# A two-layer graph attention kernel: the residual-plus-bias add on VectorE, and one product of the second projection moved

## The chip, the cores and the metric

The kernel runs on 1 core of one Trainium2 chip. The metric is the device time of a whole execution in microseconds (us). Engines are written as the profile does: PE is TensorE (PEld its weight loads), DVE is VectorE, ACT is ScalarE, POOL is GpSimd, SP is SyncE, which here only issues DMAs.

## The reference, cut to what matters

32 graphs of 512 nodes with 512 features each. The input is normalised and rectified, goes through two graph attention layers under a mask made of the adjacency matrix, and is added back to the input:

```python
h = jnp.maximum(_layernorm(x, axis=-1), 0.0)
x = x + gnn(adj, h, ...)                        # the residual

def gat_layer(x, mask, W, a_src, a_dst, bias, concat):
    xl = (x @ W).reshape(B, N, H, F)            # projection
    asrc = einsum('bnhf,hf->bnh', xl, a_src); adst = ...
    e = leaky_relu(asrc[:, :, None, :] + adst[:, None, :, :], 0.2)
    attn = softmax(where(mask[..., None], e, NEG_INF), axis=1)
    out = einsum('bsdh,bshf->bdhf', attn, xl)   # gather
    return (heads joined, or their mean) + bias

mask = (adj > 0) | eye(N)
h = elu(gat_layer(x, mask, W1, ..., b1, concat=True))    # 4 heads of 256
out = gat_layer(h, mask, W2, ..., b2, concat=False)      # 1 head of 512
```

The part that the change touches is `x + out + b2` at the end of each graph, and the order of the matrix products of `h @ W2`.

## The kernel before, in words

All data are float32 but the masks. The 512 nodes of a graph lie as 4 tiles of 128 partitions. The kernel is a pipeline over the graphs: iteration i of the main loop (L457) does, in this order on PE, the first projection of graph i+1 (`project1`, L306, `pxl`), then the second gather of graph i-1 (`gather2`, L414, `po` of L427) and the second projection of graph i (`project2`, L371, `pxm`), and then the first gather of graph i+1 (`gather1`, L325, `po` of L333). Between these products stand small transposes: of the normalised x of graph i+2 (`pht`, L187), of masks (`pm`, L208), and of softmax rows (`pas`, `prr`, L227). PE's order is the program's own (L456). DVE, ACT, POOL and SP get theirs from the scheduler, which works on what depends on what and may place an instruction well ahead of the line that wrote it. Each engine and SP's queue of DMAs run their instructions strictly in that order.

The attention of a head (class `Soft`) goes through all engines. `first(h)` (L254) makes the scores on ACT (L263), masks them on DVE (L266), takes exponentials on ACT (L270) and ends in a column `r`. `turn(h)` (L282) transposes `r` on PE (`prr`, L227), copies it out of PSUM on DVE (`rrr`, L229), writes it to DRAM (`drr`, L231) and reads it back spread over all partitions (`orr`, L233). `second(h)` (L285) makes the probabilities `p` in four passes on DVE (L292), four exponentials on ACT (L296) and two minima with the mask on DVE (L300). During one `gather2` and `project2` the heads 0 to 3 of graph i+1 go through these steps one behind the other.

`project2` multiplies by a Strassen-like scheme: 14 products (m, n), with n from 1 to 7 and m the half of the rows, each of 8 PE instructions. Products with the same accumulator (`pxm_0a`, `pxm_0b`, `pxm_0g`, `pxm_1a`, ...) add up in the same PSUM bank, and after each product the bank is read out before the next product adds to it: n = 1, 5, 6 by a copy on ACT (L399), n = 4 by a copy on ACT (L401), the others by an addition on DVE (L404). Their order is the list in L389. So product (1, 7), which adds to `pxm_1a`, waits until ACT has copied `pxm_1a` after (1, 6); (0, 4) waits until DVE has read `pxm_0a` after (0, 7); and (1, 4) until DVE has read `pxm_1a` after (1, 7).

All small transposes share two PSUM tiles in turn (tag `tp`, bufs=2), so a transpose waits until the one two places ahead has been copied out.

In `gather2` the x of the graph is loaded a second time in two tiles `xr` of two node tiles each (L421), POOL adds the bias of the second layer to each (L422, 128x1024), DVE adds the gather's PSUM result to it (L432), and SP stores it (L433). The `xr` tiles have two buffers, so a load waits for the store of the graph before.

Of the kernel before, what the change touches and what calls it, by code (L numbers as in the profile page):

```python
# [8 lines left out]
F32 = mybir.dt.float32  # L9
# [3 lines left out]
OP = mybir.AluOpType  # L13
# [3 lines left out]
P = 128  # L17
# [11 lines left out]
def tile_gat(  # L29
# [30 lines left out]
    nc = tc.nc  # L60
    B, N, D = x.shape
# [3 lines left out]
    NT = N // P  # L65
# [7 lines left out]
    work = ctx.enter_context(tc.tile_pool(name="work", bufs=2))  # L73
# [22 lines left out]
    b2_sb = const.tile([P, DO], F32, name="b2_sb")  # L96
# [57 lines left out]
    def load(b):  # L154
        XT[b] = []
        for t in range(NT):
            xt = work.tile([P, D], F32, tag="x", name=f"x{b}_{t}", bufs=4)
            nc.sync.dma_start(xt, x[b, t * P : (t + 1) * P, :])
            XT[b].append(xt)

    def load_adj(b):
        ADJ[b] = []
        for t in range(NT):
            a = work.tile([P, N], I32, tag="adj", name=f"adj{b}_{t}", bufs=2)
            nc.sync.dma_start(a, adj[b, t * P : (t + 1) * P, :])
            ADJ[b].append(a)
# [179 lines left out]
    def x2(b):  # L346

        if b < B - 1:
            return xl2

        return bass.AP(
            tensor=xl.tensor, offset=xl.offset, ap=[xl.ap[0], [DO + 2, NT], [1, DO + 2]]
        )

    def sums2(b):

        h1 = H1.pop(b)
        M = N // 2
        a11, a12 = h1[:, :KH, :M], h1[:, KH:, :M]
        a21, a22 = h1[:, :KH, M:], h1[:, KH:, M:]  # L360
        hs = work.tile([P, 3, KH, M], F32, tag="hs", name=f"hs{b}", bufs=1)
        s1, s2, s4 = (hs[:, i] for i in range(3))
        nc.vector.tensor_add(s1, a21, a22)
        nc.vector.tensor_sub(a21, a11, a21)
        nc.vector.tensor_sub(s2, s1, a11)
        nc.vector.tensor_sub(s4, a12, s2)
        LEFT[b] = {1: a11, 2: a12, 3: s4, 4: a22, 5: s1, 6: s2, 7: a21}
# [3 lines left out]
    def project2(b):  # L371
        left = LEFT.pop(b)
        v = x2(b)
        bank = {}

        def product(m, n, acc, first):
            if first:
                bank[m, acc] = psum.tile([P, 512], F32, tag="mm", name=f"pxm{b}_{m}{acc}", bufs=6)
            ps = bank[m, acc]
            for k in range(KH):  # L380
                nc.tensor.matmul(  # L381
                    ps[:, :W2H], left[n][:, k, m * P : (m + 1) * P], RIGHT[n][:, k, :],
                    start=(first and k == 0), stop=(k == KH - 1), skip_group_check=True,
                )

        def block(r, c, m):
            return v[:, 2 * r + m, c * W2H : (c + 1) * W2H]

        for m, n in (  # L389
            (0, 1), (0, 2), (0, 5), (1, 1), (0, 6), (1, 2), (1, 5),  # L390
            (0, 7), (1, 6), (0, 3), (1, 7), (0, 4), (1, 3), (1, 4),
        ):
            acc = {1: "a", 2: "g", 5: "b", 6: "a", 7: "a", 3: "b", 4: "a"}[n]
            product(m, n, acc, n in (1, 2, 5))
            ps = bank[m, acc][:, :W2H]

            if n in (1, 5, 6):
                to = {1: (0, 0), 5: (1, 1), 6: (0, 1)}[n]
                nc.scalar.activation(block(*to, m), ps, AF.Copy)  # L399
            elif n == 4:  # L400
                nc.scalar.activation(block(1, 0, m), ps, AF.Copy)  # L401
            else:
                to = block(*{2: (0, 0), 7: (1, 1), 3: (0, 1)}[n], m)
                nc.vector.tensor_add(to, ps, to)  # L404
            yield

    def cols2(b):
# [3 lines left out]

        return cols

    def gather2(b):  # L414
        p = PS2.pop(b)
        v = x2(b)
        for d in range(NT):
            if d % 2 == 0:
                xr = work.tile([P, 2, D], F32, tag="xr", name=f"xr{b}_{d}", bufs=2)
                for j in range(2):  # L420
                    nc.sync.dma_start(xr[:, j, :], x[b, (d + j) * P : (d + j + 1) * P, :])  # L421
                nc.gpsimd.tensor_tensor(  # L422
                    xr, xr, b2_sb[:, None, :].to_broadcast([P, 2, D]), op=OP.add
                )
            ps = psum.tile([P, 512], F32, tag="mm", name=f"po2{b}_{d}", bufs=6)
            for s in range(NT):
                nc.tensor.matmul(  # L427
                    ps, p[:, s, d * P : (d + 1) * P], v[:, s, 1 : DO + 1],
                    start=(s == 0), stop=(s == NT - 1),
                )  # L430
            to = xr[:, d % 2, :]
            nc.vector.tensor_tensor(to, ps, to, op=OP.add)  # L432
            nc.sync.dma_start(out[b, d * P : (d + 1) * P, :], to)  # L433
            yield

    def step(g):

        if g is not None:
            next(g, None)

    def rest(g):
        for _ in g or ():
            pass
# [9 lines left out]
    def second_layer(b):  # L453
        return Soft(b, 2, cols2(b), lambda h, p: PS2.__setitem__(b, p))

    with tc.manual_schedule(engines={mybir.EngineType.PE}):  # L456
        for i in range(-1, B + 1):  # L457

            front = i + 2 < B
            nm = norm(i + 2) if front else None  # L460
            if front:
                load(i + 2)
                load_adj(i + 2)
                step(nm)
            s1 = None
            if i + 1 < B:
                s1 = Soft(i + 1, 1, cols1, lambda h, p, b=i + 1: PS1.__setitem__((b, h), p))
                mt = turned_masks(i + 1)
                for n, _ in enumerate(project1(i + 1)):
                    if n == 0 and late:  # L470
                        late.turn(0)
                        late.second(0)
                    step(mt)
                    if n == 2 and 0 <= i:
                        sums2(i)
                    if n == 3:
                        s1.columns(0)
                    if n == 4:
                        s1.rows(0)
                    if n == 5:  # L480
                        s1.first(0)
                    if n == 7:
                        s1.columns(1)
                        s1.first(1)
            else:
                if i < B:
                    sums2(i)
                    late.turn(0)
                late.second(0)
            late = None  # L490
            last = i == B - 1


            plan = {}
            if s1:
                plan = {
                    1: lambda: s1.rows(1),
                    3: lambda: (s1.turn(0), s1.first(2)),
                    4: lambda: s1.second(0),
                    9: lambda: (s1.turn(1), s1.first(3)),  # L500
                    10: lambda: s1.second(1),
                    13: lambda: s1.turn(2),
                    14: lambda: s1.second(2),
                    16: lambda: s1.turn(3),
                }
            g2 = gather2(i - 1) if i >= 1 else iter(())
            c2 = project2(i) if 0 <= i < B else iter(())
            order = [g2] * 4 + [c2] * 14
            if last:
                order = [g2] * 2 + [c2] * 14 + [g2] * 2  # L510
            for n, g in enumerate(order, 1):
                next(g, None)
                if n in plan:
                    plan.pop(n)()
                if n in (2, 6, 10, 14):
                    step(nm)
                if last and n == 16:
                    late = second_layer(i)
                    late.columns(0)
                if last and n == 17:  # L520
                    late.rows(0)
                    late.first(0)
            rest(nm)
            if last:
                late.turn(0)
            if 0 <= i < B and not last:
                late = second_layer(i)
                late.columns(0)
            if i + 1 < B:
                for n, _ in enumerate(gather1(i + 1)):  # L530
                    if n == 1:
                        s1.second(3)
                    if n == 2 and late:
                        late.rows(0)
                        late.first(0)
                    if n == 4 and front:
                        masks(i + 2)
# [29 lines left out]
```

## Time and profile before

| what | us |
|---|---|
| median of 3 runs | 3373.64 (3365.79 to 3383.51) |
| the profiled execution | 3373.38 |
| its span, first to last instruction | 3371.6 |
| PE busy | 3184.9 (94% of the span) |
| DVE busy | 2324.9 (69%) |
| ACT busy | 1791.2 (53%) |
| POOL busy | 218.9 (6%) |
| mean share of full TensorE clock granted | 0.973 |

[...] Below, "iteration g" is the stretch from the first matmul of the second gather of graph g to that of graph g+1; in it `project2` works on graph g+1 and the heads of graph g+2 go through their steps. Idle time of the other engines costs nothing unless PE waits for what they do late.

### The profile page before, as it was taken

The numbers are of one execution on the slowest core, as the hardware profiler recorded it, in microseconds if no ns is written. First come the engines' busy times: TensorE is split into PE (matmuls) and PEld (weight loads), VectorE is DVE, ScalarE is ACT, GpSimd is POOL, SyncE is SP. The second block draws the span as 40 slices with busy tenths as digits, with TensorE's granted clock in tenths as the row PEclk, the third lists the DMA queues.
The fourth block names the chain that finished last, engine by engine and source line by source line (L and its number), as shares of the span: only waits on it lengthen the run. The fifth ranks groups of instructions, "written<-read, shape, count | busy, mean of one in ns | idle before, by whom it ended". The sixth has DMA issues, their size and how long they took to land.

```text
span 3371.6 us, 35481 instructions
## 1 busy us (share of the span) xinstructions
PE 3184.9 (94%) x12032; PEld 2158.0 (64%) x12032; DVE 2324.9 (69%) x5099; ACT 1791.2 (53%) x3873; POOL 218.9 (6%) x102
## 2 busy tenths in 40 slices
PE   5899999999999999999999999999999999999986
PEld 4566676676666666666666676666666666666654
DVE  6677676677776677666677766676766776667762
ACT  2555655455555555555545555555554455555551
POOL 0000000000000000000000000000000000000000
PEclk8899999999999999999999999999999999999998
DMA  5112222222222222222222322122322222221121
GB/s 178 49 56 79 91 94 80 70 73 79 91 94 85 72 67 79 91 94 82 69 72 73 94 87 83 58 82 85 94 85 66 73 76 91 85 80 52 66 72 47
DMA packets 121462, 269.38 MB, mean 80 GB/s; under 512 B 15552, under 2 KB 22592, under 8 KB 121280
## 3 DMA queue, kind: packets, MB, share of 16 engines
q1 hardware_dynamic: 121280, 267.12, 24.7%
q8 instruction: 94, 1.54, 0.2%
q14 instruction: 88, 0.72, 0.1%
HBM read 232.53 MB, written 34.54 MB: 79 GB/s over the span
## 4 chain that ended last, share of the span: by engine, by line
PE 49%; DMA 19%; ACT 15%; DVE 14%; issue 1%; SPq 0%; POOL 0%; ACTq 0%; DVEq 0%
PE po L333 26%; PE pxl L313 12%; ACT l L263 6%; ACT l L270 6%; DMA oas<-das 6%; DMA orr<-drr 5%; PE pxm_1a L381 5%; DVE p L300 4%; DVE p L292 3%; DVE l L266 3%; DMA adj<-in_adj_dram 3%; PE pxm_0a L381 2%; DMA das<-ras 2%; DMA drr<-rrr 2%; PE pxm_1b L381 2%
## 5 line engine op out<-in xcount | busy, mean ns | idle before, releaser
L313 PE MATMUL pxl<-w_sb,ht 128*128 128x258 f32 x4096 | 933.9, 384 | 2.3 <-DMA w_sb<-in_L_gnn_W_dram 2.3
L333 PE MATMUL po<-p,xl 128*128 128x512 f32 x2048 | 889.3, 593 | 0.0
L266 DVE CUSTOM_DVE_ANT_0 l<-l,mt 128x512 f32<-128x512 f32 x640 | 462.4, 745 | 575.8 <-ACT l L263 573.6
L313 PEld LDWEIGHTS pxl<-w_sb,ht 128*128 128x128 f32 x4096 | 768.6, 191 | 127.0 <-issue 14.8
L333 PEld LDWEIGHTS po<-p,xl 128*128 128x128 f32 x2048 | 387.1, 190 | 473.3 <-issue 443.5
L263 ACT ACTIVATE l<-oas,sc 128x512 f32<-128x512 f32 x640 | 432.8, 710 | 267.4 <-DMA oas<-das 265.6
L296 ACT ACTIVATE p<-p,lo 128x512 f32<-128x512 f32 x640 | 436.1, 717 | 250.2 <-DVE p L292 249.3
L292 DVE SCALAR_TENSOR_TENSOR p<-orr,lo 128x512 f32<-128x512 f32 x640 | 447.9, 746 | 99.0 <-DMA orr<-drr 97.1
L270 ACT ACTIVATE l<-l,low 128x512 f32<-128x512 f32 x640 | 454.7, 711 | 104.8 <-DVE low L266 104.8
L427 PE MATMUL po<-xl,p 128*128 128x512 f32 x1024 | 461.8, 597 | 19.8 <-DVE p L300 19.8
L317 ACT ACTIVATE xl<-pxl 128x258 f32<-128x258 f32 x512 | 188.7, 381 | 535.7 <-PE pxl L313 535.1
L300 DVE TENSOR_TENSOR p<-p,m 128x1024 f32<-128x1024 f32 x320 | 439.0, 1393 | 1.2 <-ACT p L296 1.1
L422 POOL TENSOR_TENSOR xr<-xr,b_sb 128x1024 f32<-128x1024 f32 x64 | 185.5, 2898 | 2592.4 <-DMA drr<-rrr 1128.2
L427 PEld LDWEIGHTS po<-xl,p 128*128 128x128 f32 x1024 | 188.6, 191 | 231.9 <-issue 202.7
L381 PE MATMUL pxm_1a<-w_sb,h 128*128 128x257 f32 x768 | 214.9, 428 | 88.3 <-ACT xl L399 88.3
L339 ACT ACTIVATE e<-po,b_sb 128x512 f32<-128x512 f32 x256 | 170.3, 677 | 162.2 <-PE po L333 159.1
L381 PEld LDWEIGHTS pxm_1a<-w_sb,h 128*128 128x128 f32 x768 | 159.8, 212 | 121.3 <-ACT xl L399 95.4
L381 PE MATMUL pxm_0a<-w_sb,h 128*128 128x257 f32 x768 | 200.3, 406 | 4.5 <-ACT xl L399 4.2
L341 DVE SCALAR_TENSOR_TENSOR h<-po,b_sb,e 128x512 f32<-128x512 f32 x256 | 191.2, 747 | 7.8 <-PE po L333 0.5
L381 PEld LDWEIGHTS pxm_0a<-w_sb,h 128*128 128x128 f32 x768 | 159.7, 209 | 49.5 <-issue 14.7
L340 DVE TENSOR_SCALAR e<-e 128x512 f32<-128x512 f32 x256 | 107.6, 421 | 65.8 <-ACT e L339 65.7
L381 PE MATMUL pxm_0b<-w_sb,hs 128*128 128x257 f32 x512 | 121.9, 380 | 0.0
(77 smaller groups left out, 2330.9 us busy)
## 6 DMA issues: line engine op xcount, KB each, us to landing
orr<-drr SPq DMA_DIRECT2D x160, 512.0 KB
x<-in_x_dram SPq DMA_DIRECT2D x128, 256.0 KB
adj<-in_adj_dram SPq DMA_DIRECT2D x128, 256.0 KB
xr<-in_x_dram SPq DMA_DIRECT2D x128, 256.0 KB
oas<-das SPq DMA_DIRECT2D x64, 512.0 KB
out_dram<-xr SPq DMA_DIRECT2D x128, 256.0 KB
oas<-das SPq DMA_DIRECT2D x32, 256.0 KB
w_sb<-in_L_gnn_W_dram SPq DMA_DIRECT2D x8, 512.0 KB
```

The costliest lines, as they stand in the source:

```text
L263: nc.scalar.activation(e, self.asr[i][:, j, :], AF.Prelu, bias=ad[:, d : d + 1], alpha=SLOPE)
L266: nc.vector.tensor_tensor_reduce(out=e, in0=e, in1=MASKT[self.b][:, d, :], scale=-1.0, scalar=BIG, op0=OP.add, op1=OP.min, accum_out=low[: ...
L270: nc.scalar.activation(e, e, AF.Exp, bias=low[:, d : d + 1], scale=-1.0, accum_out=tot[:, d : d + 1])
L292: nc.vector.scalar_tensor_tensor(p[:, u, :], rr[:, 0, :], lo[:, 0, j, u : u + 1], rr[:, 1, :], op0=OP.add, op1=OP.max,)
L296: nc.scalar.activation(p[:, u, :], p[:, u, :], AF.Exp, bias=lo[:, 1, j, u : u + 1])
L300: nc.vector.tensor_tensor(pp, pp, MASK[self.b][:, t : t + 2, :], op=OP.min)
L313: nc.tensor.matmul(ps[:, :W], ht[:, k, t * P : (t + 1) * P], w1_sb[:, k, h, :], start=(k == 0), stop=(k == KT - 1),)
L317: nc.scalar.activation(xl[:, t, h, :], ps[:, :W], AF.Copy)
L333: nc.tensor.matmul(ps, xl[:, s, h, 2 + f * P : 2 + (f + 1) * P], p[:, s, :], start=(s == 0), stop=(s == NT - 1),)
L341: nc.vector.scalar_tensor_tensor(H1[b][:, g, :], ps, bias, e, op0=OP.add, op1=OP.max)
L381: nc.tensor.matmul(ps[:, :W2H], left[n][:, k, m * P : (m + 1) * P], RIGHT[n][:, k, :], start=(first and k == 0), stop=(k == KH - 1), skip_ ...
L427: nc.tensor.matmul(ps, p[:, s, d * P : (d + 1) * P], v[:, s, 1 : DO + 1], start=(s == 0), stop=(s == NT - 1),)
```

## The change

The bias add moves from POOL (`nc.gpsimd`) to DVE (`nc.vector`), in two instructions of 128x1024 for each graph as before, and is written in the program behind a step of the first projection; the loads of `xr` are written at the start of the iteration instead of inside `gather2`. In the list of products (0, 4) and (1, 7) change places.

```diff
         for m, n in (
             (0, 1), (0, 2), (0, 5), (1, 1), (0, 6), (1, 2), (1, 5),
-            (0, 7), (1, 6), (0, 3), (1, 7), (0, 4), (1, 3), (1, 4),
+            (0, 7), (1, 6), (0, 3), (0, 4), (1, 7), (1, 3), (1, 4),
         ):
...
+    def residual(b):
+
+        XR[b] = []
+        for d in range(0, NT, 2):
+            xr = work.tile([P, 2, D], F32, tag="xr", name=f"xr{b}_{d}", bufs=2)
+            for j in range(2):
+                nc.sync.dma_start(xr[:, j, :], x[b, (d + j) * P : (d + j + 1) * P, :])
+            XR[b].append(xr)
+
+    def residual_bias(b):
+        for xr in XR[b]:
+            nc.vector.tensor_add(xr, xr, b2_sb[:, None, :].to_broadcast([P, 2, D]))
+
     def gather2(b):
         p = PS2.pop(b)
         v = x2(b)
+        xrs = XR.pop(b)
         for d in range(NT):
-            if d % 2 == 0:
-                xr = work.tile([P, 2, D], F32, tag="xr", name=f"xr{b}_{d}", bufs=2)
-                for j in range(2):
-                    nc.sync.dma_start(xr[:, j, :], x[b, (d + j) * P : (d + j + 1) * P, :])
-                nc.gpsimd.tensor_tensor(
-                    xr, xr, b2_sb[:, None, :].to_broadcast([P, 2, D]), op=OP.add
-                )
...
-            to = xr[:, d % 2, :]
+            to = xrs[d // 2][:, d % 2, :]
...
+            if i >= 1:
+                residual(i - 1)
...
+                    if n == 4 and 1 <= i:
+                        residual_bias(i - 1)
...
                 late.second(0)
+                residual_bias(i - 1)
```

On PE, at the end of `project2` in an iteration of the steady state (here iteration 8; `pxm_1a` reading `hs` is (1, 6) and stands just ahead, `pxm_0b` is (0, 3), then (1, 7), (0, 4), (1, 3) and (1, 4)), there stands before:

```order
L381 MATMUL pxm_0b<-w_sb,hs_6442 128x257 x4
L187 MATMUL pht_3_6803<-identf,x_3_6345 128x128 x4
L381 MATMUL pxm_1a<-w_sb,h_6218 128x257 x4
L381 MATMUL pxm_0a<-w_sb,h_6218 128x257 x4
L227 MATMUL prr_1_3_6819<-identf,r_1_3_6735 8x128
L381 MATMUL pxm_1b<-w_sb,hs_6442 128x257 x4
L381 MATMUL pxm_1a<-w_sb,h_6218 128x257 x4
```

And the same place on PE after the change:

```order
L381 MATMUL pxm_0b<-w_sb,hs_6448 128x257 x4
L187 MATMUL pht_3_6803<-identf,x_3_6345 128x128 x4
L381 MATMUL pxm_0a<-w_sb,h_6218 128x257 x4
L381 MATMUL pxm_1a<-w_sb,h_6218 128x257 x4
L227 MATMUL prr_1_3_6819<-identf,r_1_3_6735 8x128
L381 MATMUL pxm_1b<-w_sb,hs_6448 128x257 x4
L381 MATMUL pxm_1a<-w_sb,h_6218 128x257 x4
```

(1, 7) has one more product ahead of it, and only (1, 3) and a transpose are left between it and (1, 4).

On DVE, in the same iteration, from the read-out of (1, 2) to the passes that make `p` of head 1, there stands before:

```order
L404 TENSOR_TENSOR xl_83<-pxm_1g,xl_83 128x257
L174 BN_AGGR mv_6981<-stats_6980 128x2
L274 TENSOR_TENSOR low_1_3_6715<-low_1_3_6715,tot_1_3_6716 128x4
L276 TENSOR_TENSOR r_1_3_6735<-sc_1_1_6549,low_1_3_6715 128x4
L277 SCALAR_TENSOR_TENSOR r_1_3_6735<-sc_1_1_6549,low_1_3_6715 128x4
L173 BN_STATS stats_6980<-x_2_6968 128x6
L174 BN_AGGR mv_6981<-stats_6980 128x2
L404 TENSOR_TENSOR xl_83<-pxm_0a,xl_83 128x257
L292 SCALAR_TENSOR_TENSOR p_1_1_6744<-orr_1_1_6713,lo_1_0_6467 128x512 x4
```

And the same stretch on DVE after the change (L427 is now the bias add):

```order
L404 TENSOR_TENSOR xl_83<-pxm_1g,xl_83 128x257
L174 BN_AGGR mv_6981<-stats_6980 128x2
L427 TENSOR_TENSOR xr_2_6996<-xr_2_6996,b_sb 128x1024
L274 TENSOR_TENSOR low_1_3_6715<-low_1_3_6715,tot_1_3_6716 128x4
L276 TENSOR_TENSOR r_1_3_6735<-sc_1_1_6557,low_1_3_6715 128x4
L277 SCALAR_TENSOR_TENSOR r_1_3_6735<-sc_1_1_6557,low_1_3_6715 128x4
L173 BN_STATS stats_6980<-x_2_6968 128x6
L174 BN_AGGR mv_6981<-stats_6980 128x2
L404 TENSOR_TENSOR xl_83<-pxm_0a,xl_83 128x257
L292 SCALAR_TENSOR_TENSOR p_1_1_6744<-orr_1_1_6713,lo_1_0_6473 128x512 x4
```

The second of the two bias adds stands there; it belongs to the next graph, since the scheduler brings it forward to where its x has been loaded. The first stands some 25 rows earlier, between the second and the third mask pass (L266) of head 2.

Further on, DVE's rows behind the passes of head 1, up to the sum for the normalisation of graph i+2, were before:

```order
L300 TENSOR_TENSOR p_1_1_6744<-p_1_1_6744,m_6306 128x1024 x2
L229 COPY rrr_1_2_6780<-prr_1_2_6778 8x128
L404 TENSOR_TENSOR xl_83<-pxm_0b,xl_83 128x257
L404 TENSOR_TENSOR xl_83<-pxm_1a,xl_83 128x257
L173 BN_STATS stats_6980<-x_3_6970 128x6
L174 BN_AGGR mv_6981<-stats_6980 128x2
L176 TENSOR_SCALAR rstd_6990<-mv_6981 128x4
```

And are on DVE after the change:

```order
L300 TENSOR_TENSOR p_1_1_6744<-p_1_1_6744,m_6306 128x1024 x2
L229 COPY rrr_1_2_6780<-prr_1_2_6778 8x128
L404 TENSOR_TENSOR xl_83<-pxm_0b,xl_83 128x257
L173 BN_STATS stats_6980<-x_3_6970 128x6
L174 BN_AGGR mv_6981<-stats_6980 128x2
L176 TENSOR_SCALAR rstd_6990<-mv_6981 128x4
L404 TENSOR_TENSOR xl_83<-pxm_1a,xl_83 128x257
```

The read-out of `pxm_1a` after (1, 7) has moved behind three small instructions. On SP the loads of `xr` stand where they stood, each behind the store that frees its buffer; the one move there is that the spread read `orr` of head 2 now goes ahead of the write `drr` of head 3. POOL keeps only the power function of the normalisation (L177).

## Rows read from the trace of the kernel before

**Rows 1.** The page: its span.

```profile
span 3371.6 us, 35481 instructions
```

**Rows 2.** Sums by stretch: iterations 1 and 8, and 29 iterations.

```profile
core 0: us, PE busy (x) PEld busy (x) DVE busy (x) ACT busy (x) POOL busy (x), PEclk, DMA share, GB/s
354.83:452.96 98.13, 97.43 (x377) 66.18 (x376) 70.47 (x155) 55.62 (x124) 7.06 (x3) 1.00 0.26 84
...
1059.40:1160.86 101.46, 99.11 (x377) 67.35 (x376) 71.12 (x155) 55.79 (x122) 7.26 (x3) 0.98 0.26 81
249.63:3211.87 2962.24, 2870.62 (x10905) 1948.01 (x10904) 2076.92 (x4480) 1622.74 (x3516) 197.65 (x86) 0.98 0.25 80
```

**Rows 3.** Waits by pair: us in total, times, longest us.

```profile
PE pxm_1a L381 <- ACT xl L399: 88.3, 30, 4.4
```

**Rows 4.** PE in order of time, iteration 8: start, duration; [idle before, releaser].

```profile
1095.25 3.00 PE L381 MATMUL pxm_1a<-w_sb,h 128*128 128x257 f32 x8 [2.35 <-ACT xl L399]
1098.05 2.63 PE L381 MATMUL pxm_0a<-w_sb,h 128*128 128x257 f32 x8
1100.51 0.27 PE L227 MATMUL prr<-identf,r 128*8 128x128 f32 x1
```

**Rows 5.** The chain of waits in order of time, iteration 8: start, us.

```profile
1088.43 1.21 DMA drr<-rrr
1089.66 3.74 DMA orr<-drr
...
1094.93 0.28 ACT xl L399
...
1095.25 3.00 PE pxm_1a L381 x8
...
1100.79 1.74 PE pxm_1b L381 x8
```

**Rows 6.** ACT in order of time, iteration 8.

```profile
1094.20 0.72 ACT L296 ACTIVATE p<-p,lo 128x512 f32<-128x512 f32 x1 [2.63 <-DVE p L292]
```

**Rows 7.** DVE in order of time, iteration 8.

```profile
1078.38 0.74 DVE L266 CUSTOM_DVE_ANT_0 l<-l,mt 128x512 f32<-128x512 f32 x1 [1.43 <-ACT l L263]
...
1083.08 1.22 DVE L300 TENSOR_TENSOR p<-p,m 128x1024 f32<-128x1024 f32 x1
...
1084.83 3.38 DVE L300 TENSOR_TENSOR p<-p,m 128x1024 f32<-128x1024 f32 x1
...
1093.42 2.74 DVE L292 SCALAR_TENSOR_TENSOR p<-orr,lo 128x512 f32<-128x512 f32 x4 [0.52 <-DMA orr<-drr]
...
1098.35 0.27 DVE L229 COPY rrr<-prr 8x128 f32<-8x128 f32 x1
```

**Rows 8.** POOL in order of time, iteration 8.

```profile
1075.67 2.89 POOL L422 TENSOR_TENSOR xr<-xr,b_sb 128x1024 f32<-128x1024 f32 x1 [75.62 <-DMA drr<-rrr]
1083.78 3.35 POOL L422 TENSOR_TENSOR xr<-xr,b_sb 128x1024 f32<-128x1024 f32 x1 [5.21 <-DMA xr<-in_x_dram]
```

**Rows 9.** Groups by line: xcount | busy us, mean ns | idle before, releasers.

```profile
L300 DVE TENSOR_TENSOR p<-p,m 128x1024 f32<-128x1024 f32 x320 | 439.0, 1393 | 1.2 <-ACT p L296 1.1
...
L366 DVE TENSOR_TENSOR hs<-h,hs 128x1024 f32<-128x1024 f32 x32 | 39.2, 1226 | 1.1
...
L177 POOL TENSOR_TENSOR rstd<-rstd,half 128x4 f32<-128x4 f32 x32 | 32.8, 1024 | 528.0 <-DVE rstd L176 516.6 <-DVE sc L321 11.4
```

**Rows 10.** PE in order of time, iteration 1.

```profile
389.04 2.01 PE L381 MATMUL pxm_1a<-w_sb,h 128*128 128x257 f32 x8 [0.70 <-ACT xl L399]
```

**Rows 11.** DVE in order of time, iteration 1.

```profile
370.85 0.68 DVE L432 TENSOR_TENSOR xr<-po,xr 128x512 f32<-128x512 f32 x1
```

**Rows 12.** POOL in order of time, iteration 1.

```profile
370.44 2.71 POOL L422 TENSOR_TENSOR xr<-xr,b_sb 128x1024 f32<-128x1024 f32 x1 [76.03 <-DMA drr<-rrr]
```

**Rows 13.** DVE in order of time, at the program's start.

```profile
39.42 0.42 DVE L136 SCALAR_TENSOR_TENSOR j<-w_sb,a 128x256 f32<-128x256 f32 x1
...
39.76 2.57 DVE L136 SCALAR_TENSOR_TENSOR j<-w_sb,a 128x256 f32<-128x256 f32 x1
```

More of the change, by code (lines that the diff above doesn't have):

```diff
@@ L412, in cols2 @@
         return cols
+    XR = {}
+    def residual(b):
[8 more added lines that the diff above has]
+            nc.vector.tensor_add(xr, xr, b2_sb[:, None, :].to_broadcast([P, 2, D]))
     def gather2(b):
```

## The prediction, made before the changed kernel was run

> **What bounds the kernel now.** I read the page first, then the sums by stretch, then PE's waits, and then one iteration on each engine in order of time. The page gives the span of 3371.6 us [rows 1]; the sums show PE busy for 2870.62 of 2962.24 us [rows 2], so only what PE loses can be won. Iteration 1 shows the floor: 98.13 us, of which PE is busy 97.43, at the full granted clock of 1.00; its one loss that counts is a wait of 0.70 us [rows 2, 10]. The 29 iterations from 249.63 to 3211.87 last 2962.24 us, or 102.15 each, at a mean clock of 0.98 [rows 2]. Against the floor, 29 x 97.43 = 2825.5, they lose 136.8 us. Of that 2962.24 - 2870.62 = 91.6 is idle PE, and 2870.62 - 2825.5 = 45.1 is the same work at a lower clock.
>
> Nearly all idle time is one wait: product (1, 7) on `pxm_1a` waits for ACT's copy after (1, 6), 30 times, 88.3 us [rows 3]. In iteration 8 it is 2.35 us, and behind it the clock is down: (1, 7) takes 3.00 us and (0, 4) 2.63, where an undisturbed product takes 1.74 from start to start [rows 4, 5].
>
> Why is ACT late? The copy takes 0.28 us, but stands in ACT's order behind the first exponential of head 1, and that waited 2.63 us for DVE's L292 [rows 5, 6]. L292 waited for the spread read `orr`, and the chain runs back through `orr` (3.74 us) and `drr` (1.21 us) to DVE's copy `rrr` [rows 5, 7]. That copy stands behind the second L300, which took 3.38 us where its twin took 1.22 [rows 7]. In that time POOL's bias add ran, from 1083.78 to 1087.13 [rows 8]; L300 ended 1084.83 + 3.38 = 1088.21, about one L300 after POOL was done. The mean of 320 L300 is 1393 ns [rows 9], so (1.393 - 1.22) x 320 = 55 us, some 26 such collisions of 2.16 us, nearly one per iteration. So the root of PE's wait is POOL's add, off every critical path itself.
>
> **The change part by part.**
>
> *POOL's two adds of a graph go.* In iteration 8 the chain from L300 on comes 3.38 - 1.22 = 2.16 us earlier; the copy that PE waits for would end at 1094.93 + 0.28 - 2.16 = 1093.05.
>
> *DVE gets the two adds.* Nothing in the trace adds the broadcast bias on DVE; the nearest row is L366, also two float32 inputs and 128x1024, at 1.226 us [rows 9]. I take 1.23 each, 2.45 per iteration. The first stands before the third mask pass of head 2. POOL began that add at 1075.67 [rows 8], so x has landed by then, when DVE has just done the pass ahead of it; and before the fourth pass DVE idles 1.43 us [rows 7], which takes the add up. Cost 0 to 0.3 us. The second stands between `rrr` of head 1 and L292 of head 1, while `drr` and `orr` travel. DVE waited 0.52 us at the end of that stretch [rows 7], so the add delays L292 by at most 1.23 - 0.52 = 0.7 us. From both sides: the copy ends between 1093.05 and 1094.05; without that cover (both adds wholly on the chain) at 1095.5. I take 0.5 us of delay, hence 1093.55, between the ends, since both idle times are rows of the very stretch.
>
> *The loads of xr.* SP's order keeps them behind the stores that free their buffers, so they are no earlier. No gain, no cost; every spread read issued behind them waits as before. `orr` of head 2 goes ahead of `drr` of head 3, which no PE row waits for.
>
> *(0, 4) goes ahead of (1, 7).* PE came to the place at 1095.25 - 2.35 = 1092.90 [rows 4]. (0, 4) now fills 1.74 us, so (1, 7) is due at 1094.64, some 1.1 us after the copy has ended (0.6 to 1.6). The wait goes, and with it the fall of the clock, since a wait of 0.70 us left the clock at 1.00 over its whole iteration [rows 2, 10]. Iteration 1 bears this out from the other side: it lost 0.70 us without the swap, and 1.74 is more than that. (0, 4) itself needs DVE's read-out of `pxm_0a`, which stands just ahead of L292: ready by 1091.8, a microsecond before it is due.
>
> *What is late next.* The transpose `prr` of head 3 uses the PSUM tile that `rrr` of head 2 has to empty. That copy ended at 1098.35 + 0.27 = 1098.62, which is 5.20 us after L292 began [rows 7]; PE's transpose came at 1100.51 and did not wait [rows 4]. Now L292 begins at about 1093.42 - 2.16 + 0.5 = 1091.76 and the copy ends at 1096.96, while PE is due at 1094.64 + 1.74 = 1096.38: a new wait of 0.6 us (0.1 to 0.8 by the bounds above). I take 0.5 per iteration as the mean, since in iterations like 1 there is less. DVE's read-out of `pxm_1a` after (1, 7), now behind three small instructions, is hidden by (1, 3) at 1.74 us, but it stands right behind L176, when POOL's L177 runs (1.02 us, [rows 9]). Held up for all of that time, as L300 was by POOL's add, it would make (1, 4) wait up to 1.0 us more: 30 x 1.0 = 31 us. The nearest row is L432, which like the read-out has one input in PSUM and one in SBUF: beside POOL's add it took its usual 0.68 us [rows 11, 12]. So I take 0 and keep the 31 for the range.
>
> [...]
>
> *The start.* Two of POOL's adds ran beside the weight products L136 and held one at 2.57 us instead of 0.42 [rows 13], the other alike: 4.3 us of a DVE stretch for which PE waits. The two adds stand there on DVE too, 2.45 us, partly while DVE has nothing else. Gain 1.9 to 4.3; I take 3.
>
> **Sum.** 29 x (102.15 - 97.43 - 0.5) = 122.4; the one such wait ahead of that window, 88.3 / 30 - 0.5 = 2.4; the start 3. Together 127.8 us off the profiled execution's 3373.38 (span 3371.6 and 1.8 around it): 3245.6. The median of the runs shown is 0.3 above the profiled one, so 3246. With the residual at 0 instead of 0.5, and 4.3 at the start, 3229; with 1.0 and 1.9, 3262. That is the forecast's own range.
>
> **Rivals.**
>
> *The adds land on the chain.* DVE has no slack in the stretch, and both push everything behind them. The copy ends at 1095.5, PE waits 0.9 us at (1, 7); L292 begins at 1093.7, the copy `rrr` of head 2 ends at 1098.9, and the transpose, due at 1097.3, waits 1.6 more. 2.5 us in two pieces, 30 x 2.5 = 75: 3373.4 - 136.8 - 2.9 - 3 + 75 = 3306. For it: DVE would be nearly without a pause there. Against: the 1.43 and 0.52 us idle.
>
> *POOL is not the cause.* L300 is slow for another reason and stays so; only the swap acts. The mean wait 88.3 / 30 = 2.94 falls to 1.2 us, 36 us in all, with the clock still falling in perhaps a third of the iterations (15 us of the 45): 3373.4 - 142.7 + 51 = 3282, and up to 3320 with the adds' cost. Against: 1083.78 and 1087.13 frame the slow L300.
>
> *Slower.* DVE runs in order, so the first add, before the third mask pass, holds up every chain if its x lands late. In the trace it lands just in time (1075.67). Behind 1.43 us of idle and 1.1 us of margin every further microsecond goes to PE. To lose more than the present 4.7 us per iteration with 0.5 and a fallen clock (45.1 / 29 = 1.6) already counted, x must land some 5 us later than now. At 8 us later: 8 - 2.5 + 0.5 + 1.6 = 7.6 per iteration, 29 x 2.9 = 84 us more, 3457. Against: SP's order has the loads where they were, behind the same stores.
>
> *It does not do what it says.* The loads are not earlier; were the rest as ineffective, 3373. Against: the orders of PE, DVE and POOL do change.
>
> **How the numbers follow.** Forecast 0.75; adds on the chain 0.12; POOL not the cause 0.06; no change 0.03; slower 0.04. About 0.5% (17 us) is what can be told from no change, so the first three cases are faster: 0.93, the same 0.03, slower 0.04. The range takes the forecast's own, the 31 us of L177 on its upper side (3277) and the nearer part of the rivals: 3227 to 3295.
>
> **What would show it.** L300 at one duration near 1.22 us and its mean with it; no wait of `pxm_1a` on ACT's L399; the iterations at 98 us with the clock at 1.00; the bias adds at 1.23 us; a short wait of `prr` on `rrr`. The forecast is wrong if (1, 7) still waits for ACT, or if (1, 4) or `prr` waits over 1 us per iteration, or if the first add waits for its x.

## The result, and the profile after

The changed kernel took 3245.09 us (median of 4 runs, 3243.96 to 3247.49) where the kernel before took 3378.57 beside it (4 runs, 3365.79 to 3393.66): a ratio of 0.9604, 95% interval 0.9562 to 0.9647. Repeated in two further sessions (chips 9 and 8) it was 0.9594 (0.9564 to 0.9625) and 0.9591 (0.9563 to 0.9619). The prediction was 3246 us, with a range of 3227 to 3295. Since the kernel before varies from 3379 to 3395 us from one session and chip to another, experiments are compared below by their ratio to it, or with a kernel that ran beside them.

The page of the changed kernel; its first line answers [rows 1]:

```profile
span 3242.4 us, 35403 instructions
...
PE 3142.2 (97%) x12032; PEld 2125.1 (66%) x12032; DVE 2282.4 (70%) x5163; ACT 1785.5 (55%) x3873; POOL 33.2 (1%) x38
```

The sum over the same 29 iterations as the last of [rows 2], with the columns given there:

```profile
243.41:3084.53 2841.12, 2826.91 (x10905) 1914.81 (x10904) 2034.78 (x4536) 1616.98 (x3515) 28.20 (x28) 1.00 0.26 83
```

One iteration lasts 2841.12 / 29 = 97.97 us instead of 102.15. PE is idle in (2841.12 - 2826.91) / 29 = 0.49 us of it instead of 3.16, and its busy time has fallen from 2870.62 to 2826.91 us at a granted clock of 1.00: the same work, no longer partly at a lower clock (0.98 in the mean before [rows 2]).

The waits by pair (us in total, times, longest us); the last row answers [rows 3]:

```profile
DVE p L292 <- DMA orr<-drr: 81.4, 75, 4.9
...
PE pxm_1a L381 <- DVE xl L404: 10.6, 19, 0.8
...
PE prr L227 <- ACT ht L188: 2.2, 7, 0.3
...
PE pxm_1a L381 <- ACT xl L399: 1.2, 2, 0.9
```

The wait for ACT's copy has gone from 88.3 us to 1.2. What is left is small and elsewhere: product (1, 4) waits for DVE's read-out of `pxm_1a`. The groups by line; the first answers the first of [rows 9]:

```profile
L300 DVE TENSOR_TENSOR p<-p,m 128x1024 f32<-128x1024 f32 x320 | 382.6, 1216 | 0.6 <-ACT p L296 0.4
...
L427 DVE TENSOR_TENSOR xr<-xr,b_sb 128x1024 f32<-128x1024 f32 x64 | 76.9, 1203 | 6.1 <-DMA xr<-in_x_dram 4.5 <-DMA drr<-rrr 1.0 <-issue 0.2
...
L404 DVE TENSOR_TENSOR xl<-pxm_1a,xl 128x257 f32<-128x257 f32 x32 | 13.4, 418 | 4.8 <-PE pxm_1a L381 4.8
```

L300 is at 1216 ns instead of 1393, so none of 3.38 us is left, and the new add takes 1203 ns. Iteration 8 again, first the chain that ended last in it, which answers [rows 5]:

```profile
1053.71 1.14 DVE p L300
...
1055.08 1.20 DMA drr<-rrr
...
1056.30 3.93 DMA orr<-drr
...
1060.25 2.74 DVE p L292 x4
...
1066.71 0.43 DVE xl L404
...
1067.19 2.00 PE pxm_1a L381 x8
```

The chain is the old one, with the same round trip through DRAM, but it starts with an L300 of usual length. It no longer runs through ACT; its end is the read-out L404 that (1, 4) waits for. The engines in order of time in the same iteration, DVE (as [rows 7]), ACT (as [rows 6]), PE (as [rows 4]) and POOL:

```profile
1044.47 1.22 DVE L427 TENSOR_TENSOR xr<-xr,b_sb 128x1024 f32<-128x1024 f32 x1 [0.83 <-DMA xr<-in_x_dram]
...
1053.64 1.22 DVE L300 TENSOR_TENSOR p<-p,m 128x1024 f32<-128x1024 f32 x1
...
1057.21 1.18 DVE L427 TENSOR_TENSOR xr<-xr,b_sb 128x1024 f32<-128x1024 f32 x1
...
1059.47 0.39 DVE L404 TENSOR_TENSOR xl<-pxm_0a,xl 128x257 f32<-128x257 f32 x1
1060.25 2.74 DVE L292 SCALAR_TENSOR_TENSOR p<-orr,lo 128x512 f32<-128x512 f32 x4 [0.39 <-DMA orr<-drr]
...
1065.18 0.27 DVE L229 COPY rrr<-prr 8x128 f32<-8x128 f32 x1
...
1065.71 0.67 DVE L173 BATCH_NORM_STATS2 stats<-x 128x6 f32<-128x512 f32 x1
...
1066.71 0.42 DVE L404 TENSOR_TENSOR xl<-pxm_1a,xl 128x257 f32<-128x257 f32 x1
```

```profile
1061.04 0.72 ACT L296 ACTIVATE p<-p,lo 128x512 f32<-128x512 f32 x1 [2.78 <-DVE p L292]
1061.67 0.36 ACT L399 ACTIVATE xl<-pxm_1a 128x257 f32<-128x257 f32 x1
```

```profile
1061.16 1.91 PE L381 MATMUL pxm_0a<-w_sb,h 128*128 128x257 f32 x8
1062.90 1.90 PE L381 MATMUL pxm_1a<-w_sb,h 128*128 128x257 f32 x8
1064.64 0.27 PE L227 MATMUL prr<-identf,r 128*8 128x128 f32 x1
1064.75 1.91 PE L381 MATMUL pxm_1b<-w_sb,hs 128*128 128x257 f32 x8
1067.19 2.00 PE L381 MATMUL pxm_1a<-w_sb,h 128*128 128x257 f32 x8 [0.53 <-DVE xl L404]
```

```profile
1066.95 1.01 POOL L177 TENSOR_TENSOR rstd<-rstd,half 128x4 f32<-128x4 f32 x1 [97.00 <-DVE rstd L176]
```

The second add is over at 1057.21 + 1.18 = 1058.39, and the passes L292 start at 1060.25, when the spread read `orr` has landed: the add lies wholly inside the round trip. ACT's copy ends at 1062.03, 0.87 us before (1, 7) at 1062.90. The read-out at 1066.71 takes its usual 0.42 us, but it starts 0.24 us ahead of POOL's L177, as do all 27 read-outs that overlap with an L177 in this trace; so whether L177 would hold it is not put to the test here.

### The profile page after: what moved, and what is told of

Read it like the earlier page. It is cut to its first block, busy times and chain, and to the rows that moved or that the text cites. A ratio compares the mean times of both kernels' runs of the same rounds, so it can differ in the third digit from the quotient of the medians.

```text
span 3242.4 us, 35403 instructions
## 1 busy us (share of the span) xinstructions
PE 3142.2 (97%) x12032; PEld 2125.1 (66%) x12032; DVE 2282.4 (70%) x5163; ACT 1785.5 (55%) x3873; POOL 33.2 (1%) x38
## 4 chain that ended last, share of the span: by engine, by line
PE 64%; DMA 13%; DVE 12%; ACT 10%; issue 1%; SPq 0%; POOL 0%; ACTq 0%; DVEq 0%
PE po L333 27%; PE pxl L313 18%; PE po L436 6%; ACT l L270 5%; ACT l L263 5%; DMA oas<-das 4%; PE pxm_1a L381 4%; DVE p L292 4%; DMA orr<-drr 3%; DVE p L300 3%; PE pxm_0a L381 3%; DMA adj<-in_adj_dram 2%; DVE l L266 1%; PE pxm_1b L381 1%; PE pxm_0b L381 1%; DMA das<-ras 1%
## 5 line engine op out<-in xcount | busy, mean ns | idle before, releaser
L266 DVE CUSTOM_DVE_ANT_0 l<-l,mt 128x512 f32<-128x512 f32 x640 | 426.9, 686 | 546.1 <-ACT l L263 546.1
L292 DVE SCALAR_TENSOR_TENSOR p<-orr,lo 128x512 f32<-128x512 f32 x640 | 447.6, 745 | 83.0 <-DMA orr<-drr 81.4
L300 DVE TENSOR_TENSOR p<-p,m 128x1024 f32<-128x1024 f32 x320 | 382.6, 1216 | 0.6 <-ACT p L296 0.4
L381 PE MATMUL pxm_1a<-w_sb,h 128*128 128x257 f32 x768 | 185.9, 384 | 12.2 <-DVE xl L404 10.6
L381 PE MATMUL pxm_0a<-w_sb,h 128*128 128x257 f32 x768 | 184.3, 382 | 0.1
L381 PEld LDWEIGHTS pxm_1a<-w_sb,h 128*128 128x128 f32 x768 | 142.5, 189 | 44.4 <-DVE xl L404 20.5
L381 PEld LDWEIGHTS pxm_0a<-w_sb,h 128*128 128x128 f32 x768 | 143.8, 191 | 33.8 <-issue 14.5
L381 PE MATMUL pxm_1b<-w_sb,hs 128*128 128x257 f32 x512 | 121.9, 380 | 0.0
```

The source lines that it names most:

```text
L266: nc.vector.tensor_tensor_reduce(out=e, in0=e, in1=MASKT[self.b][:, d, :], scale=-1.0, scalar=BIG, op0=OP.add, op1=OP.min, accum_out=low[: ...
L292: nc.vector.scalar_tensor_tensor(p[:, u, :], rr[:, 0, :], lo[:, 0, j, u : u + 1], rr[:, 1, :], op0=OP.add, op1=OP.max,)
L300: nc.vector.tensor_tensor(pp, pp, MASK[self.b][:, t : t + 2, :], op=OP.min)
L381: nc.tensor.matmul(ps[:, :W2H], left[n][:, k, m * P : (m + 1) * P], RIGHT[n][:, k, :], start=(first and k == 0), stop=(k == KH - 1), skip_ ...
```

## The experiments

Ratios are to the kernel before on the same chip, with 95% intervals. The two parts of the change, and a third way to deal with POOL's add, stand against each other like this:

| bias add | old order of products | (0, 4) ahead of (1, 7) |
|---|---|---|
| on POOL, whole | 1 | 0.9842 (0.9812 to 0.9873) |
| on POOL, in 8 pieces | 0.9698 (0.9671 to 0.9726) | 0.9668 (0.963 to 0.9706) |
| on DVE | 0.9613 (0.958 to 0.9646), 0.9623 (0.9598 to 0.9648) | the changed kernel, 0.959 to 0.960 |
| left out | | 0.9607 (0.958 to 0.9634) |

The exchange moves more than the two products. In every kernel of the right column the scheduler places DVE's read-out of `pxm_1a` behind the three small instructions of the statistics, in the left column ahead of them; the right column is the worth of both.

**The add on DVE without the exchange.** The changed kernel with

```diff
-            (0, 7), (1, 6), (0, 3), (0, 4), (1, 7), (1, 3), (1, 4),
+            (0, 7), (1, 6), (0, 3), (1, 7), (0, 4), (1, 3), (1, 4),
```

> The changed kernel with the old order of the products, (1, 7) ahead of (0, 4): only the move of the adds to DVE and the earlier loads stand. Theory (POOL's add beside L300 is the root of the long wait): all 320 L300 near 1.22 us; product (1, 7) waits again for ACT's copy after (1, 6), but only by the rest that the swap covered, 0.6 to 1.2 us per iteration, and the clock stays at 1.00 in most of them: 3250 to 3275 us. Rival (the swap does the work): the 2.94 us wait comes back whole and the clock falls with it, 3355 to 3375 us.

Measured: 3261.22 us beside 3391.39, ratio 0.9613. L300 is at 1219 ns, and (1, 7) waits for ACT's copy 23 times, 28.8 us, 0.96 us per iteration of idle PE in all. So taking POOL's add away is the main part, as the theory said; the rival falls. What the exchange adds on top was too small to see here, so both kernels ran once more side by side:

> The changed kernel with the old order of the products once more, now beside the changed kernel on one chip: what is the exchange of (0, 4) and (1, 7) worth once the adds are on DVE? Its ratio to before was 0.9613, with an interval that holds that of the changed kernel (0.9604, 0.9594). Theory (the traces of single executions: idle PE of 0.96 us per iteration against 0.49 and 0.55, three falls of the clock against none): 29 x (98.54 - 98.0) = 15 us more than the changed kernel, 0.3 to 0.6%. Rival (the exchange only moves the wait from (1, 7) to (1, 4)): within 0.15%.

> The changed kernel unaltered beside the old order of the products. Theory: 0.3 to 0.6% less than that one, wait of (1, 7) on ACT's copy below 2 us in all and no fall of the clock between the first and the thirtieth graph. Rival: within 0.15% of it, with as much idle PE at (1, 4) as the other has at (1, 7).

Measured: 3263.89 us (3262.97 to 3267.03, 4 runs) and 3252.94 (3246.28 to 3258.72, 5 runs); the two sets do not overlap, and the medians differ by 10.95 us, 0.34%. The wait by pair of the old order,

```profile
PE pxm_1a L381 <- ACT xl L399: 27.2, 21, 3.3
```

is 0.9 us in the other, which in turn waits 14.3 us at (1, 4): rather more than half of the wait moves, and the rest goes. The two profiled spans are 10.4 us apart: the 29 iterations hold 2852.65 - 2846.05 = 6.6 of it and the stretch ahead of them 251.82 - 245.91 = 5.9, and the end gives 2.1 back. The exchange is worth a third of a per cent once the adds are on DVE, the lower end of what I expected.

**The exchange alone.** The kernel before with the other line of the list.

> The kernel before with (0, 4) put ahead of (1, 7); POOL still makes the adds. Theory: L300 is still held to about 3.38 us some 26 times (mean near 1.39 us), so ACT's copy is as late as before; the product in between covers 1.74 us of the 2.94, which leaves 1.2 us per iteration, and what is behind the late chain (the transpose prr of head 3, product (1, 4)) may wait more: 3285 to 3320 us. Rival (the swap does the work): as fast as the changed kernel, 3245 us within 10. Rival (the adds on DVE are all): the wait only moves to other products, 3360 us or more.

Measured: 3337.05 us, ratio 0.9842; above my range. 27 of the L300 still take 3.37 to 3.39 us, and the waits are spread:

```profile
PE pxm_1a L381 <- DVE xl L404: 22.7, 29, 1.3
PE pxm_1a L381 <- ACT xl L399: 19.9, 26, 1.3
...
PE pxm_0a L381 <- DVE xl L404: 19.5, 22, 1.7
...
PE prr L227 <- ACT ht L188: 8.6, 28, 0.3
```

Idle PE is 2.57 us per iteration, not much less than the 3.16 before, but in four pieces of at most 1.7 us, and the granted clock is 1.00 in the mean of the 29 iterations, where it was 0.98 [rows 2]. I had left out the third row: DVE is so late that (0, 4), now due 1.74 us earlier, waits for its own read-out of `pxm_0a`. In the changed kernel that read-out ended at 1059.86, 1.3 us ahead of (0, 4).

**The bias add left out.** The changed kernel without the two adds.

```diff
-            nc.vector.tensor_add(xr, xr, b2_sb[:, None, :].to_broadcast([P, 2, D]))
+            pass
```

> The changed kernel with the bias add of the residual left out (output lacks b2). It prices the two adds on DVE, 2.4 us per iteration. Theory (0.5 us of them reach PE, as a wait per iteration): that wait is gone, 3228 to 3235 us. Rival 1 (DVE's idle time hides them whole and the residual wait has another source): 3242 to 3246 us, with the wait of (1, 4) still there. Rival 2 (they cost their full length): 3245 - 32 x 2.4 = 3168 us, which lies below the 97.43 us per iteration that PE needs, so PE would have to be shorter too.

Measured: 3255.9 us beside 3391.39, ratio 0.9607, the same as with the adds. Rival 1 holds, its times to be read against that chip's 3391. The waits by pair show why:

```profile
DVE p L292 <- DMA orr<-drr: 97.4, 87, 5.1
...
PE pxm_1a L381 <- DVE xl L404: 14.7, 22, 0.8
```

The wait of (1, 4) is still there, and DVE waits 16 us longer for `orr` than with the adds (81.4). The order on DVE is otherwise the same, and the 29 iterations last 2851.14 us, no less than the 2841.12 to 2846.05 of three profiles with the adds. The adds fill time in which DVE waits; my 0.5 us per iteration was not theirs.

**POOL's add in pieces.** The kernel before, old order of the products, with

```diff
-                nc.gpsimd.tensor_tensor(
-                    xr, xr, b2_sb[:, None, :].to_broadcast([P, 2, D]), op=OP.add
-                )
+                for j in range(2):
+                    for c in range(0, D, 128):
+                        nc.gpsimd.tensor_tensor(
+                            xr[:, j, c : c + 128], xr[:, j, c : c + 128],
+                            b2_sb[:, c : c + 128], op=OP.add)
```

> The kernel before with each of POOL's adds of 128x1024 cut into eight of 128x128; order of products as before. It asks whether a DVE instruction that meets POOL's add stands still until that one POOL instruction is over, or whether the two share and both run slower while POOL is at work. Theory (stands still until the instruction is over): an L300 then loses at most about a piece, 0.3 to 0.5 us and not 2.16, unless it is stopped by one piece after the other; few L300 above 2 us, mean near 1.25 us, the wait of (1, 7) below 1.5 us, 3280 to 3330 us. Rival (share of bandwidth, or the queue of pieces holds DVE for as long as the one add did): L300 still at 3 us or more some 26 times, 3365 to 3390 us.

Measured: 3289.38 us, ratio 0.9698, as the theory said; the rival falls. PE, DVE, ACT and SP run the same instructions in the same order as in the kernel before, so nothing but POOL's pieces differs. (1, 7) waits 28 times, 40.4 us. The group of L300, then one of them on DVE and POOL's pieces beside it:

```profile
L300 DVE TENSOR_TENSOR p<-p,m 128x1024 f32<-128x1024 f32 x320 | 390.9, 1243 | 0.8 <-ACT p L296 0.4
```

```profile
1066.98 1.47 DVE L300 TENSOR_TENSOR p<-p,m 128x1024 f32<-128x1024 f32 x1
```

```profile
1065.82 4.23 POOL L424 TENSOR_TENSOR xr<-xr,b_sb 128x128 f32<-128x128 f32 x4 [3.51 <-DMA xr<-in_x_dram]
```

POOL is at work from before this L300 until after it, yet L300 loses 1.47 - 1.22 = 0.25 us, once. All 32 that lost anything took 1.47 to 1.50. An eighth of 2.16 is 0.27: the hold went down with the size of POOL's instruction, and was not repeated by those behind it. The rival, a share of bandwidth or a hold for as long as the queue, had L300 at 3 us or more. POOL itself is busier (360 us in these adds), which costs nothing. The runs give the lengths, 2.16 us beside adds of 2.90 us in the mean and 0.25 us beside pieces of 0.74; by what POOL holds DVE they do not show.

The pieces and the exchange together:

> The kernel before with POOL's adds cut into eight pieces and (0, 4) put ahead of (1, 7); DVE gets no add. With the pieces alone L300 was held 0.26 us instead of 2.16, and PE still waited 1.4 us per iteration for ACT's copy. Theory (what counts is how long one POOL instruction holds DVE, and the swap covers what the round trip of the spread read leaves): idle PE 0.5 to 0.8 us per iteration, clock at 1.00 throughout, ratio to before 0.960 to 0.967, like the changed kernel. Rival (the 104 passes L266 that are each held 0.25 us, 26 us in all, reach PE): ratio 0.967 to 0.972, like the pieces alone.

Measured: 3274.09 us, ratio 0.9668, against 3248.98 for the changed kernel on that chip. The granted clock is 1.00 in the mean of the 29 iterations and L300 loses 7.3 us in all, but idle PE is 1.09 us per iteration against 0.55, and 92 of the masked passes L266 are held by 0.2 to 0.3 us, 23 us in all. The ratio alone doesn't decide, since its interval reaches into both ranges; the idle time does, and is closer to the rival. With (0, 4) ahead of (1, 7), short holds were better than long ones (0.9668 against 0.9842), and none was better still (0.959 to 0.960). That it is the holds of L266 that reach PE was not shown by itself.

**The add made twice.** The changed kernel with `for _ in range(2):` ahead of the add.

> The changed kernel with each bias add made twice on DVE (the output holds b2 twice): 2.4 us more of DVE per iteration. Leaving the adds out gave no gain (0.9607 against 0.9604 of before), so DVE's idle time ahead of L292 (1.31 us of waiting for orr in iteration 13 of the changed kernel) and ahead of the fourth mask pass hides them. Theory (hidden in waits of about 1.3 us each): the second copy of each add uses up what is left, so at most 0.3 us per iteration more reach PE, 0 to 10 us. Rival (DVE has no idle time left in these two stretches and everything behind the adds moves): 1.2 to 2.4 us per iteration, 35 to 75 us.

Measured: 3424.8 us, ratio 1.0115 (1.0074 to 1.0155): 176 us more than the changed kernel beside it, more than either theory allowed. Here is one iteration, DVE and PE in order of time:

```profile
1322.57 2.72 DVE L292 SCALAR_TENSOR_TENSOR p<-orr,lo 128x512 f32<-128x512 f32 x4
1325.22 2.34 DVE L300 TENSOR_TENSOR p<-p,m 128x1024 f32<-128x1024 f32 x2
1327.49 0.41 DVE L404 TENSOR_TENSOR xl<-pxm_0a,xl 128x257 f32<-128x257 f32 x1
```

```profile
1327.95 3.79 PE L381 MATMUL pxm_0a<-w_sb,h 128*128 128x257 f32 x8 [5.12 <-DVE xl L404]
```

With the longer adds the scheduler has put the read-out of `pxm_0a` behind L292 and L300, where in the changed kernel it stands ahead of them (1059.47 against 1060.25 above). So (0, 4) waits 5.12 us, and behind the wait its eight matmuls take 3.79 us instead of 1.91. The wait by pair over the run,

```profile
PE pxm_0a L381 <- DVE xl L404: 133.8, 28, 6.2
```

is nearly all of PE's idle time. The 29 iterations last 3021.96 us against 2843.60 in the changed kernel beside it; of these 178 us more, 119 are idle PE (135.0 against 16.0) and 59 are the same work at a lower granted clock (2886.91 against 2827.63 us busy, 0.97 against 1.00). The experiment does not price the adds, then; it shows what one place in DVE's order is worth (others moved too, but PE hardly waits for them). What more DVE work would cost in an unchanged order was not measured.

**A further exchange.** The changed kernel, the control and this on one chip:

```diff
-            (0, 1), (0, 2), (0, 5), (1, 1), (0, 6), (1, 2), (1, 5),
-            (0, 7), (1, 6), (0, 3), (0, 4), (1, 7), (1, 3), (1, 4),
+            (0, 1), (0, 2), (0, 5), (1, 1), (0, 6), (1, 2), (1, 6),
+            (0, 7), (1, 5), (0, 3), (1, 7), (0, 4), (1, 3), (1, 4),
```

> The changed kernel unaltered, beside the three others on one chip, since the kernel before took 3378.6 us on one chip and 3391.4 on another: ratio to before 0.957 to 0.965. In the trace the wait of (1, 4) on DVE's read-out of pxm_1a stays at no more than 0.77 us, 0.35 to 0.5 per iteration, and L300 at 1.22.

> The changed kernel with two more places exchanged in the order of the second projection: (1, 6) at the place of (1, 5), (1, 5) behind (0, 7), and (1, 7) ahead of (0, 4), so that two products, (0, 4) and (1, 3), stand between (1, 7) and (1, 4) and ACT's copy after (1, 6) stands ahead of the exponentials of head 1. Theory (what is left is the read-out of pxm_1a, late because its place on DVE is behind L292, which waits for the spread read orr): 1.74 us more of cover than the 0.77 that is missing, so the wait of (1, 4) goes and no other over 0.3 us comes: idle PE below 0.2 us per iteration, 29 x 0.4 = 12 us less than the changed kernel, ratio of the two 0.995 to 0.998. Rival (the copy of pxm_1b, or prr, then waits in its place): the idle time stays at 0.4 to 1 us per iteration, ratio of the two 0.998 to 1.005.

Measured: 3248.98 us (3248.01 to 3250.14, 6 runs) and 3233.91 (3230.48 to 3237.22, 6 runs), 0.9594 and 0.9549 (0.9515 to 0.9583) of before; the medians differ by 15.1 us, 0.46%. The sum over the 29 iterations of the new order, then its PE in order of time in one iteration, from (1, 7) on:

```profile
247.18:3072.91 2825.73, 2820.89 (x10905) 1917.23 (x10904) 2038.42 (x4536) 1610.17 (x3515) 28.19 (x28) 1.00 0.26 84
```

```profile
863.65 1.91 PE L381 MATMUL pxm_1a<-w_sb,h 128*128 128x257 f32 x8
865.39 1.90 PE L381 MATMUL pxm_0a<-w_sb,h 128*128 128x257 f32 x8
...
867.24 1.91 PE L381 MATMUL pxm_1b<-w_sb,hs 128*128 128x257 f32 x8
868.98 1.90 PE L381 MATMUL pxm_1a<-w_sb,h 128*128 128x257 f32 x8
```

Here (1, 7), (0, 4), (1, 3) and (1, 4) follow each other without a wait; idle PE is (2825.73 - 2820.89) / 29 = 0.17 us per iteration, and in the whole run no product waits for DVE's read-out of `pxm_1a`. So the late read-out was what was left, and this version beats both kernels. Two things changed for it, though. One more product, 1.74 us, stands between (1, 7) and (1, 4); and on DVE the read-out is ahead of the statistics again:

```profile
866.66 0.40 DVE L404 TENSOR_TENSOR xl<-pxm_1a,xl 128x257 f32<-128x257 f32 x1
866.99 0.67 DVE L173 BATCH_NORM_STATS2 stats<-x 128x6 f32<-128x512 f32 x1
```

In the changed kernel the statistics put it off by 1066.71 - 1065.71 = 1.00 us. Either is more than the 0.5 to 0.8 us that was missing, and this run doesn't part them.

## Why the prediction came out right, step by step

| term | predicted | measured in the profiled execution |
|---|---|---|
| 29 iterations | 122.4 us less | 2962.24 - 2841.12 = 121.1 |
| ahead of them | 2.4 + 3 | 249.63 - 243.41 = 6.2 |
| behind them | 0 | 1.9 |
| span | 127.8 | 3371.6 - 3242.4 = 129.2 |

- *The root: POOL's add holds L300.* Right, and shown: without POOL's add no L300 takes 3.38 us (1.226 at most in the changed kernel); in pieces of an eighth the hold is 0.25 us instead of 2.16; with the exchange alone 27 of them still take it. But it is not the whole root. POOL's adds held mask passes L266 as well, 18 of them, by 36 us in all. Iteration 11 of the kernel before, on DVE and on POOL:

```profile
1377.08 2.84 DVE L266 CUSTOM_DVE_ANT_0 l<-l,mt 128x512 f32<-128x512 f32 x1
```

```profile
1376.95 2.42 POOL L422 TENSOR_TENSOR xr<-xr,b_sb 128x1024 f32<-128x1024 f32 x1 [73.15 <-DMA xr<-in_x_dram]
```

In the 12 of the 29 iterations where both were held by over a microsecond, (1, 7) waited 4.0 us in the mean (4.26 in this one); in the 14 where only L300 was, as in iteration 8, 2.5; no run has the one hold without the other. Iteration 1, the prediction's floor, is no undisturbed one either: its L300 were free, but an L266 took 2.65 us. The sum came out even so, since it set what is left from that iteration's busy time and did not need the size of the holds.
- *The chain comes earlier by the 2.16 us.* Right. From L300's end to L292's start it is 5.21 us before [rows 7] and 1060.25 - 1054.86 = 5.39 after, nearly the same round trip.
- *The adds on DVE, 1.23 us each, delaying L292 by 0.5.* The length is right (1.203). The delay is not: L292 waits for `orr` behind the add, and without the adds nothing is gained. I set the add against the 0.52 us of idle time ahead of L292 [rows 7] alone. In the same stretch DVE had also waited for ACT:

```profile
1091.33 0.16 DVE L274 TENSOR_TENSOR low<-low,tot 128x4 f32<-128x4 f32 x1 [0.69 <-ACT tot L273]
```

Together 0.69 + 0.52 = 1.21 us, which is room for the add's 1.18; it ends 1.86 us before L292 starts.
- *The exchange covers 1.74 us.* Right: ACT's copy is 0.87 us early where I had 1.1. Without it the wait was 27.2 us, 21 times.
- *A new wait of `prr` on `rrr`, 0.5 us per iteration.* This step failed, and its size came out right by luck. `prr` of head 3 starts at 1064.64, before the copy `rrr` at 1065.18 has even begun: it doesn't use the tile I named. What it waited for in these iterations was ACT's L188, the copy of a `pht`, 7 times for at most 0.3 us; so the two PSUM tiles are not taken strictly in turn, as the description of the kernel has it. Of the 0.49 us, 10.6 / 29 = 0.37 are at (1, 4), whose read-out I called hidden by (1, 3). What I missed is the place of the read-out on DVE, counted from L292: four L292, two L300, `rrr`, another read-out and the statistics make 1066.71 + 0.42 - 1060.25 = 6.88 us. With L292 at 1091.76, as I had it, that is 1098.64, and PE is due at 1094.64 + 1.74 + 1.74 = 1098.12: the same 0.5. Of the 6.88 us the three small instructions make 1.00, so without their move there would have been nothing to wait for in this iteration; I had seen the move and priced only L177 behind it. The further exchange takes the wait away.
- *L177 doesn't hold the read-out.* The outcome is right, 418 ns in the mean, and the 31 us that I kept for it were not needed. The reason, that L432 with one input in PSUM took its usual 0.68 us beside POOL's add [rows 11, 12], was not tested on the read-out: it starts ahead of L177 each time they overlap. What speaks for the reason is the run with the pieces, where 38 read-outs lay beside an add of POOL that had begun first, and took 0.41 to 0.42 us.
- *The start, and one wait ahead of the window.* The 32 weight products L136 take 11.1 us instead of 15.4, so the 4.3 us of holds are gone. In all 6.2 instead of 5.4, but the changed kernel's 243.41 is 246.43 and 245.91 in its two other profiles, so the 0.8 us more are within what executions vary by. That the end phase gains as well I had not counted: 159.73 us before, 157.87, 157.93 and 159.21 in the three profiles after.
- *The rivals.* The adds on the chain: fell, the adds cost nothing. POOL not the cause: fell, with the adds moved alone (0.9613) and in pieces (0.9698). Late x: in all 64 adds together DVE waits 4.5 us for `xr`. No change: fell.

## What to carry to other kernels

When an engine waits, follow the chain back until an instruction is longer than its twin, and look which other engine was at work in just that time; the culprit may be on no path itself. Then count over all iterations which instructions it lengthened, since one iteration may show only some of them. An add that moved to a busier engine was free here because it landed where that engine waited, for a round trip and for another engine, which is seen from what ended the idle times around it and not from busy shares. After a chain has been brought forward, count every read-out that stands behind it in the engine's order, from the chain's own start, against the product that needs it; that sum was to be had before, and an order of products made with it in mind gave another 0.46%.

## What the runs showed of the hardware that was not expected

- The hold of a DVE instruction went with the size of POOL's: 2.16 us beside adds of 128x1024, which took 2.90 us in the mean, and 0.25 beside pieces of 128x128, which took 0.74. The pieces next in POOL's queue did not prolong it.
- Held were, above all, L300 and L266, with two inputs in SBUF: 26 and 18 times by the whole adds, of 43 and 99 that lay beside one, and 32 and 104 times by the pieces. Of the read-outs L404 and the sums with the gather's result, with one input in PSUM, 38 and 30 lay beside POOL's pieces, and none was slower than usual (0.42 and 0.68 us). That the place of the inputs decides it was not shown by itself.
- Four waits of at most 1.7 us per iteration went with a granted clock of 1.00 in the mean in the kernel with the exchange alone; one of 2.35 us [rows 4] was followed by a clock of 0.50 (from 1097 to 1098), and the 13 us with the one of 5.12 us had 0.74. The length of the wait alone does not tell: in the kernel before, iteration 13 lost the clock behind 2.00 us (0.50 from 1605 to 1607) and iteration 17 kept it behind 2.34 (1.00 from 2016.5 to 2019).

```profile
1603.76 2.93 PE L381 MATMUL pxm_1a<-w_sb,h 128*128 128x257 f32 x8 [2.00 <-ACT xl L399]
...
2015.89 2.01 PE L381 MATMUL pxm_1a<-w_sb,h 128*128 128x257 f32 x8 [2.34 <-ACT xl L399]
```

- In the kernel with the exchange alone the 29 iterations have 24 us less of busy PE than before (2870.62 to 2846.31) and only 17 us less of idle PE (91.6 to 74.4): the wait cut into short ones was worth more in busy time, at a clock of 1.00 instead of 0.98, than by itself. Not all busy time above the changed kernel's is the clock, though: that kernel has 19 us more (2846.31 against 2826.91) with the clock at 1.00 in both.
